# Gelu and GpSimd units of the FFN left out of the last three slots of a fused gated cross-attention layer and put into its end list

## The chip, the cores and the metric

The kernel runs on one core of a Trainium2 chip. A core has five engines that run their own instruction queues and wait for each other with semaphores: TensorE (PE, matrix products, with PEld for its weight loads), VectorE (DVE), ScalarE (ACT), GpSimd (POOL) and SyncE (SP, which here issues all DMA transfers). The metric is the device time of one execution in microseconds (us). Before the change the median of three runs is 2996.57 us, from 2995.82 to 2997.93.

## The reference

One layer of gated cross-attention with a gated, quantised feed-forward network (FFN), on 32 sequences of 224 tokens of width 512. The context has 750 tokens of width 384 for each sequence.

```
x = x + tanh(g_xattn) * attention(layernorm(x), ctx, mask, Wq, Wkv)     # 16 heads of 32
x = x + tanh(g_ffn)   * ffn(layernorm(x), w1, b1, w2, b2)               # 512 -> 2048 -> 512

def bitlinear(x, w, b):
    xq = act_quant(rmsnorm(x))     # each row scaled by its largest value to -128..127, rounded
    wq = weight_quant(w)           # each weight to -1, 0 or 1, by the mean size of all
    return xq @ wq.T + b

ffn(x) = bitlinear(gelu(bitlinear(x, w1, b1)), w2, b2)     # gelu in its exact form
```

The softmax is over the 750 context tokens; a masked query row gets equal weights. Both feed-forward products work on rounded numbers, so before each of them a row needs its root mean square, its largest value and a rounding.

## The kernel before

**Steps and slots.** The attention is cut into 128 steps: 32 sequences times 4 groups of 4 heads. A step has six slots. The three even ones (k = 0, 2, 4) compute the scores for the maxima of the *next* step (`maxima`, line 322), the three odd ones the weights of *this* step (`weights`, line 379). `weights` writes the scores minus the maximum into PSUM (tiles `se`), takes one exponential on ScalarE over 125 x 1792 numbers (tile `p`), and lets GpSimd add the results up (tile `acc`, one addition for u = 0, two for u = 1 and u = 2). There is one PSUM tile for scores, so the scores of slot k + 1 wait until the exponential of slot k has read its own. `minus_max` (line 349) makes the maxima on VectorE after slot 4, and `turn_max` (line 368) turns them with TensorE (tile `pn`) and copies them on ScalarE into `nT`, which the scores of the next step take as an operand. `values` and `sums` (lines 412 and 426) multiply the weights of the step before with the values and add up their sums, both into a tile `po`; `finish` scales the result on GpSimd (tile `yo`) and `store` writes it to `o_d` in memory.

**FFN units.** The FFN works on 28 pairs of 128-row tiles, numbered 0 to 27. `ffn_units` (line 571) cuts a pair into small named units: `load`, `add`, `stats`, `rsqrt`, `norm`, `max`, `sa0` to `sa2`, `grid`, `bias`, `round` and `turn` for the pair, and then for each tile t of two `b` (first product and bias on VectorE, four column blocks, PSUM tiles `ph`), `gelu`, `square`, `hm` (largest value, two halves), `sb0` to `sb2` (scales), `cgrid`, `cround`, `cturn` (a DMA transpose), `c` (second product) and `out`. The numbers of a row go to an integer grid by a multiplication and an added constant (`grid`, `cgrid`), are rounded into bf16 on ScalarE (`round`, `cround`; tiles `xq`, the reused `xc`, and `hq`) and transposed (`xT`, `hT`).

**What orders them.** Every engine works in the order in which the program issues its instructions. In the steps, `Ffn.fill` (line 872) is called once in each slot with the room that is left on TensorE, ScalarE and VectorE, and takes the first units that fit and are `ready` (line 863): a unit must wait some slots after the unit before it and for the units that `behind` names. In the last step but one (n = N - 2 = 126) this is the last call of all. After it `Ffn.drain` (line 910) orders everything that is left, the last step's attention (`top` for `turn_max`, `w0` to `w2`, `val`, `fin0`, `sto0`, `vlast`, `fin1`, `sto1`) among the rest of the FFN units, by a list of costs (`TAKES_US`, line 792). It picks, among what can start within 2 us of the earliest, the unit with the longest work behind it. In the drain a Gelu is held back until the last step's exponentials are issued (line 855), since Gelu and exponential need different tables on ScalarE. In a slot of a step, `b_gelu` (line 686) issues the Gelu and then an exponential of one element a row, `warm`, which brings the exponential's table back:

```
            act.activation(h, h, AF.Gelu)
            if not draining:

                act.activation(warm, magic, AF.Exp)
```

Pairs 26 and 27 use buffers that the attention no longer needs: `xo` for their rows, `wq_sb` and `wkv_sb` for the hidden numbers of pair 26. Names such as `p_3_0` mean the tile p of head group 3 (of the last sequence), u = 0; `h_0` of pair 25 is its tile 0.

Of the kernel before, what the change touches and what calls it, by code (L numbers as in the profile page):

```python
# [24 lines left out]
def flamingo_gated_layer(  # L25
# [18 lines left out]
    class Ordered:  # L44


        def __init__(self, engine):
            self.engine = engine
# [140 lines left out]
    N = len(steps)  # L189
# [178 lines left out]
    def turn_max(n):  # L368
        b, g = steps[n]
        pn = ps_m.tile([P, NQ, CP], BF16, tag="m", name=f"pn_{b}_{g}")  # L370
        for t in range(NQ):
            pe.transpose(
                pn[:, t, :], nbs[n % 2][:, t].rearrange("p j r -> p (j r)"), identb[:CP, :CP]
            )
        nT = smp.tile([P, S], BF16, tag="nT", name=f"nT_{b}_{g}")
        act.copy(nT, pn.rearrange("p t n -> p (t n)"))
        nT_of[b, g] = nT
# [442 lines left out]
        }.items()  # L820
    }

    class Ffn:

        def __init__(self):
            self.slot = 0
            self.parts = []
            self.next = 0  # L830
            self.at = {}

        def behind(self, pair, name):

# [27 lines left out]

        def ready(self, pair, unit):
            name, lag, after = unit[:3]
            lag = lag if not draining else 0
            if after is not None:
                at = self.at.get((pair, after))
                if at is None or self.slot < at + lag:
                    return False
            return all(at in self.at for at in self.behind(pair, name))  # L870
# [39 lines left out]
        def drain(self, more):  # L910

            draining.append(True)
            free = {"PE": 0.0, "ACT": 0.0, "DVE": 4.3, "POOL": 5.0, "SP": 0.0}
            end = {}

            def takes(name):
                kind = name.rstrip("0123456789")
                return TAKES_US.get(kind) or TAKES_US[kind + name[-1]]  # L920

            self.parts.insert(0, [NF, more])
            while self.next < NF:
                self.parts += [[self.next, part] for part in ffn_units(self.next)]
                self.next += 1
            left = {}

            def rank(at):

                if at not in left:  # L930
                    left[at] = 0.0
                    left[at] = sum(us for _, us in takes(at[1])[0]) + max(
                        (rank(x) for x in behind if at in behind[x]), default=0.0
                    )
                return left[at]

            behind = {
                (pair, u[0]): [(pair, u[2] or "")] + self.behind(pair, u[0])
                for pair, units in self.parts for u in units
            }  # L940

            def course(at, way):

                t = max(
                    [end.get(x, 0.0) for x in behind[at]
                     if x[1].rstrip("0123456789") not in ORDER_ONLY or x[1][:-1] != at[1][:-1]],
                    default=0.0,
                )
                t = begin = max(t, free[way[0][0]])
                for engine, us in way:  # L950
                    t = max(t, free[engine]) + us
                return begin, t

            while self.parts:
                self.slot += 10
                found = []
                for part in self.parts:
                    for unit in part[1]:
                        if self.ready(part[0], unit):
                            at = part[0], unit[0]  # L960
                            way = min(
                                takes(unit[0]), key=lambda way: course(at, way)[1]
                                + 1.0 * sum(us for engine, us in way if engine == "DVE"),
                            )
                            found.append((course(at, way)[0], -rank(at), part, unit, way))
                soon = min(f[0] for f in found) + 2
                t, _, part, unit, way = min((f for f in found if f[0] <= soon), key=lambda f: f[1])
                part[1].remove(unit)
                self.at[part[0], unit[0]] = self.slot
                small[0] = {"DVE": dve, "POOL": gp}.get(way[-1][0], act)  # L970
                unit[6]()
                for engine, us in way:
                    t = max(t, free[engine])
                    free[engine] = t + (QUEUE_US[unit[0].rstrip("0123456789")] if engine == "SP" else us)
                    t += us
                end[part[0], unit[0]] = t
                self.parts = [p for p in self.parts if p[1]]
            return end
# [47 lines left out]
    ffn = Ffn()  # L1026
# [5 lines left out]
    for n in range(N - 1):  # L1032
        b, g = steps[n]
        nxt = steps[n + 1]
        last = steps[n - 1] if 0 < n else None
        slots = [[] for _ in range(6)]
        quick = []

        def put(k, us, fn, first=False):
            slots[k].append((us, fn))  # L1040
            if first:
                quick.append(fn)

        def put_values(*ks):

            if v_left:
                at = v_left.pop(0)
                for i, k in enumerate(ks):
                    put(k, 2.7 / len(ks), lambda i=i: v_piece(*at, i if len(ks) > 1 else None))

        put(0, 0.2, lambda: turn_max(n), first=True)
        if last:
            put(2, 2.7, lambda: (values(*last), sums(*last)), first=True)
            put(5, 0.0, lambda: store(*last), first=True)
        if n + 2 < N:
            ks = k_units(*steps[n + 2]) if n else first_k
            if n:
                put(0, 1.9, ks[0])
            put(1, 1.9, ks[1])
        if g == 2 and b + 2 < B:  # L1060
            put(0, 0.0, lambda: load_y(b + 2, 3, 0))
            put(2, 0.0, lambda: load_y(b + 2, 3, 1))
            put(4, 0.0, lambda: load_y(b + 2, 3, 2))
        if g == 3 and b + 2 < B:
            put(0, 0.0, lambda: load_x(b + 2))
        if n in V_MORE:
            put_values(V_MORE[n])
        if n == 0:
            put(3, 1.7, lambda: centre(2 * P, D))
        if n < 2:  # L1070
            put(5, 1.5, q0[n + 2])
        lent = v_left[0] if v_left else None
        put_values(4)
        whole = slots[4][-1][1] if lent else None
        if g < 2:
            put_values(3, 5)
        more = b + 1 < B
        if more and g == 0:
            norm, qs = q_units(b + 1)
            put(0, 0.0, norm[0], first=True)  # L1080
            put(2, 0.0, norm[1], first=True)
            put(4, 0.0, norm[2], first=True)
        if more and g == 1:
            put(1, 0.0, norm[3], first=True)
            put(5, 0.0, lambda: load_xT(b + 1))
        if more and g > 1:
            put(3, 1.5, qs[2 * g - 4])
            put(5, 1.5, qs[2 * g - 3])
        for k in range(6):
            if k % 2 == 0:  # L1090
                maxima(*nxt, k // 2)
            else:
                if k == 3 and last:
                    finish(*last)
                weights(b, g, k // 2)
            if k == 4:
                minus_max(n + 1)

            used = sum(us for us, _ in slots[k])
            early = [unit for us, unit in slots[k] if unit in quick]  # L1100
            for unit in early:
                unit()
            if wunits:
                if k in (1, 3, 5):
                    wunits.pop(0)()
            else:
                some = ffn.fill(
                    (PE_ROOM[k % 2] - used, (1.1, 2.2)[k % 2], 1.7),
                    (n - (k < 5)) // NG if n else 0,
                )  # L1110
                if k == 0 and not some and lent is not None:

                    v_piece(*lent, 0)
                    slots[4] = [
                        (1.35, lambda: v_piece(*lent, 1)) if unit is whole else (us, unit)
                        for us, unit in slots[4]
                    ]
            for us, unit in slots[k]:
                if unit not in quick:
                    unit()  # L1120
# [50 lines left out]
```

## Time and profile before

| what | value |
|---|---|
| median of three runs | 2996.57 us |
| profiled execution: time of its own | 2990.66 us |
| profiled execution: span, first to last instruction | 2988.9 us |
| mean granted clock of TensorE | 0.991 |
| busy: PE, DVE, ACT, POOL | 97%, 58%, 47%, 70% of the span |
| last exponential of step N - 2 | 2888.03 to 2889.69 us |
| last exponential of the last step | 2904.88 to 2906.55 us |

Times in the profile count from the first instruction. Nearly all instructions carry line 52, the helper that records them, so they are told apart by engine and tile names: `p<-se` on ACT is the exponential, `acc<-acc,p` on POOL the sums, `h<-h` on ACT a Gelu, `ACT_TABLE_LOAD` a change of ScalarE's function table. In an order of time a row gives the start, the length, engine, operation, output and input, and in square brackets how long the engine had been idle and what ended that. In the chain of work that ended last, each row is a piece that the end hung on. In a table of stretches, each engine's busy time stands with its number of instructions, in the order PE, PEld, DVE, ACT, POOL; then come the granted TensorE clock, the share of DMA time and GB/s.

The last step and the end list take the last 100 us or so of the span. There TensorE is no longer busy throughout: its wait for transposed tiles of the second FFN product alone comes to 24.4 us after 2889 us.

### The profile page before, as it was taken

Reading aid. Unit: us, or ns where it says so; the run is one execution under the profiler, and the core shown is the slowest. Engines: PE = TensorE matmul, PEld = TensorE weight load, DVE = VectorE, ACT = ScalarE, POOL = GpSimd, SP = SyncE. Lnnn points to the kernel's source line nnn. Section 1 sums busy time; section 2 is a strip of 40 time slices with the busy share of each in tenths; the row PEclk is TensorE's granted clock in tenths of the full one; section 3 lists DMA queues with packets and bytes.
Section 4 is the critical chain, followed back from the end, with each engine's and each line's share of the span. In section 5 each row is a group of like instructions: output and inputs, shape, how many; then the busy total and the mean of one; then the engine's idle time right before and its main releaser. Section 6 shows DMA issues by size and latency. Waiting matters only on the chain.

```text
span 2988.9 us, 62964 instructions
## 1 busy us (share of the span) xinstructions
PE 2891.5 (97%) x26814; PEld 1839.9 (62%) x26814; DVE 1725.5 (58%) x2588; ACT 1417.8 (47%) x1438; POOL 2081.6 (70%) x2727
## 2 busy tenths in 40 slices
PE   8999999999999999999999999999999999999976
PEld 5666566666666666666666666666666666666643
DVE  5576555655555565556555555654655655556545
ACT  2344454544545455445445454553543554545444
POOL 3566767767777777767667777767767777687674
PEclk9999999999999999999999999999999999999987
DMA  5433223123222212221222222223122222321213
GB/s 152 106 95 98 54 57 79 35 59 73 53 58 63 58 48 70 65 68 32 57 72 53 58 61 64 46 58 75 44 49 65 48 69 63 69 74 27 46 45 79
DMA packets 376697, 190.03 MB, mean 64 GB/s; under 512 B 283104, under 2 KB 340576, under 8 KB 376288
## 3 DMA queue, kind: packets, MB, share of 16 engines
q1 hardware_dynamic: 376416, 186.02, 25.8%
q8 instruction: 209, 3.42, 0.5%
q14 instruction: 72, 0.59, 0.1%
HBM read 119.86 MB, written 29.39 MB: 50 GB/s over the span
## 4 chain that ended last, share of the span: by engine, by line
PE 82%; ACT 10%; POOL 3%; DVE 3%; issue 1%; DMA 1%; POOLq 0%; ACTq 0%; SPq 0%; DVEq 0%
PE po L52 17%; PE pk L52 14%; PE se L52 14%; PE sm L52 12%; PE pv_None L52 8%; ACT p L52 7%; PE ph L52 6%; PE pv L52 6%; PE pq L52 3%; DVE mx L52 2%; ACT L52 2%; POOL acc L52 1%; ACT h L52 1%; PE pn L52 1%; POOL r_a L52 1%
## 5 line engine op out<-in xcount | busy, mean ns | idle before, releaser
L52 POOL TENSOR_TENSOR acc<-acc,p 125x896 f32<-125x896 f32 x510 | 1066.0, 2090 | 325.7 <-ACT p L52 304.2
L52 DVE TENSOR_REDUCE mx<-sm 112x4 f32<-112x2000 f32 (+1 forms) x384 | 861.0, 2242 | 664.5 <-PE sm L52 662.6
L52 ACT ACTIVATE p<-se 125x1792 f32<-125x1792 f32 x384 | 639.1, 1664 | 759.0 <-PE se L52 701.6
L52 PE MATMUL pk<-y,wkv_sb 128*128 128x375 f32 x1536 | 538.3, 486 | 2.0 <-DMA y<-in_ctxT 2.0
L52 PE MATMUL sm<-kT,qT 32*112 32x500 f32 (+1 forms) x4096 | 426.7, 508 | 31.6 <-ACT p L52 22.7
L52 POOL TENSOR_TENSOR acc<-p 125x896 f32<-125x896 f32 x128 | 268.3, 2096 | 244.4 <-ACT p L52 244.3
L52 PEld LDWEIGHTS pk<-y,wkv_sb 128*128 128x128 f32 x1536 | 277.8, 189 | 174.4 <-issue 34.5
L52 PE MATMUL se<-qT,kT 32*125 32x224 f32 x6144 | 359.5, 348 | 0.0
L52 PE MATMUL po<-p,v 125*32 125x224 f32 x6144 | 318.1, 355 | 0.0
L52 PE MATMUL pv<-wkv_sb,y 128*125 128x256 f32 x1248 | 311.0, 385 | 0.0
L52 PEld LDWEIGHTS se<-qT,kT 32*125 32x125 f32 x6144 | 295.5, 183 | 0.0
L52 PEld LDWEIGHTS sm<-kT,qT 32*112 32x112 f32 x4096 | 159.2, 170 | 190.1 <-ACT p L52 138.7
L52 PEld LDWEIGHTS po<-p,v 125*32 125x32 f32 x6144 | 186.9, 110 | 119.5 <-issue 44.0
L52 PEld LDWEIGHTS pv<-wkv_sb,y 128*125 128x125 f32 x1248 | 223.2, 188 | 52.3 <-issue 17.8
L52 ACT COPY kT<-pk 128x375 f32<-128x375 f32 x256 | 120.3, 470 | 278.8 <-PE pk L52 278.0
L52 PE MATMUL pv_None<-wkv_sb,y 128*125 128x256 f32 x1056 | 250.9, 387 | 0.0
L52 PEld LDWEIGHTS pv_None<-wkv_sb,y 128*125 128x125 f32 x1056 | 191.2, 187 | 89.0 <-issue 59.7
L52 PE MATMUL po<-w2q,hT 128*128 128x256 fp8e4 x1792 | 222.1, 280 | 24.4 <-DMA hT<-hq 24.4
L52 DVE SCALAR_TENSOR_TENSOR h<-ph,qa_am,b_sb 128x512 f32<-128x512 f32 x216 | 158.9, 745 | 139.0 <-PE ph L52 111.1
L52 PE MATMUL ph<-w1q,xT 128*128 128x512 fp8e4 x896 | 226.1, 384 | 4.8 <-DMA xT<-xc 4.8
L52 PE MATMUL pq<-xTb,wq_sb 128*128 128x224 f32 x1024 | 221.4, 359 | 0.4 <-DVE wq_sb L52 0.4
L52 PEld LDWEIGHTS <-hT 128*128 128x128 bf16 x1792 | 171.8, 100 | 76.6 <-issue 27.1
(131 smaller groups left out, 2863.1 us busy)
## 6 DMA issues: line engine op xcount, KB each, us to landing
y<-in_ctxT SPq DMA_DIRECT2D x90, 375.0 KB, 4.7
x<-in_x SPq DMA_DIRECT2D x32, 448.0 KB, 4.0
xTb<-in_xT SPq DMA_DIRECT2D x32, 448.0 KB, 3.7
o_d<-yo SPq DMA_DIRECT2D x512, 28.0 KB, 1.9
xg<-in_x SPq DMA_DIRECT2D x26, 512.0 KB, 3.8
og<-o_d SPq DMA_DIRECT2D x26, 512.0 KB, 4.4
out<-xg SPq DMA_DIRECT2D x52, 256.0 KB, 2.2
wa<-in_w1T SPq DMA_DIRECT2D x8, 512.0 KB, 5.6
```

Source lines behind the costliest of these rows:

```text
L52: return lambda *args, **kw: tc.keep_in_program_order(build(*args, **kw))
```

## The change

In the slots k = 3, 4 and 5 of the step n = N - 2, a unit whose name without its digits is in `NOT_LAST` is not ready. It stays in the list of the FFN and is ordered by the drain instead. The flag is cleared when the drain begins. The names are Gelu and units that run on GpSimd. Nothing is left out of the computation.

```
+    NOT_LAST = "gelu", "add", "rsqrt", "grid", "bias", "cgrid", "sb"
...
     class Ffn:
...
             self.at = {}
+            self.closing = False
...
         def ready(self, pair, unit):
             name, lag, after = unit[:3]
+            if self.closing and name.rstrip("0123456789") in NOT_LAST:
+                return False
...
             draining.append(True)
+            self.closing = False
...
             else:
+                ffn.closing = n == N - 2 and k > 2
                 some = ffn.fill(
```

More of the change, by code (lines that the diff above doesn't have):

```diff
@@ L821, in flamingo_gated_layer @@
     }
+    NOT_LAST = "gelu", "add", "rsqrt", "grid", "bias", "cgrid", "sb"
     class Ffn:
@@ L831, in __init__ @@
             self.at = {}
+            self.closing = False
         def behind(self, pair, name):
@@ L864, in ready @@
             name, lag, after = unit[:3]
+            if self.closing and name.rstrip("0123456789") in NOT_LAST:
+                return False
             lag = lag if not draining else 0
@@ L914, in drain @@
             draining.append(True)
+            self.closing = False
             free = {"PE": 0.0, "ACT": 0.0, "DVE": 4.3, "POOL": 5.0, "SP": 0.0}
@@ L1106, in flamingo_gated_layer @@
             else:
+                ffn.closing = n == N - 2 and k > 2
                 some = ffn.fill(
```

## The prediction

> **What bounds the kernel now.** The page comes first. TensorE (PE) is busy for 97% of the span, but an average can hide the end, and the change touches only the last step, so the second view is the chain of work that ended last, from 2888 us on. The third is each engine's order of time over the last 100 us, the fourth a table of stretches with the granted clock.
>
> From the page:
>
> ```profile
> span 2988.9 us, 62964 instructions
> PE 2891.5 (97%) x26814; PEld 1839.9 (62%) x26814; DVE 1725.5 (58%) x2588; ACT 1417.8 (47%) x1438; POOL 2081.6 (70%) x2727
> ```
>
> From the chain (start, us, what):
>
> ```profile
> 2888.03 1.66 ACT p L52
> 2889.71 1.28 ACT L52
> 2891.00 1.91 ACT h L52
> 2892.93 1.28 ACT L52
> 2894.22 0.20 ACT warm L52
> 2894.43 0.24 ACT nT L52
> 2894.71 2.13 PE se L52 x19
> ...
> 2903.66 2.08 POOL acc L52
> ...
> 2910.07 1.37 POOL xc L52 x2
> ...
> 2911.46 1.16 ACT xc L52
> 2912.64 2.42 DMA xT<-xc
> ```
>
> The reader is to see that between the last exponential of step N-2 and the first scores of the last step the chain runs through ScalarE (ACT) alone: a table load, the Gelu of one FFN tile, a table load back, the one-element exponential, and only then the copy nT that the scores wait for. After that it runs over the sums of the weights on GpSimd (POOL) to the quantisation of pair 26 there, and from this through ACT and a DMA to PE.
>
> From PE's, POOL's and ACT's order of time:
>
> ```profile
> 2886.73 0.41 PE L52 MATMUL se<-nT,ones 3*125 3x448 bf16 x4 [0.53 <-DVE mx L52]
> 2889.57 0.26 PE L52 MATMUL pn<-identb,nb 112*128 112x112 bf16 x2
> 2894.71 0.64 PE L52 MATMUL se<-nT,ones 3*125 3x448 bf16 x4 [4.88 <-ACT nT L52]
> 2900.07 0.55 PE L52 MATMUL po<-acc,ones 125*32 125x224 f32 x8
> 2889.83 4.23 POOL L52 TENSOR_TENSOR acc<-acc,p 125x896 f32<-125x896 f32 x2 [2.24 <-ACT p L52]
> 2911.46 1.15 ACT L52 ACTIVATE xc<-xc,magic 128x1024 bf16<-128x1024 f32 x1 [4.92 <-POOL xc L52]
> ```
>
> PE turned the maxima (pn) by 2889.83 and then sat for 4.88 us until nT came. The scores after this idle are slow, 0.64 us where 2886.73 shows 0.41 for the same four matmuls. The stretches say why: in the column PEclk (the fraction after the five engines) the clock is 1.00, and half of that after the idle.
>
> ```profile
> 2886.00:2890.00 4.00, 3.30 (x31) 1.97 (x31) 3.79 (x11) 1.96 (x2) 1.76 (x2) 1.00 0.27 106
> 2895.00:2898.00 3.00, 3.00 (x36) 1.93 (x35) 0.00 (x0) 1.03 (x1) 0.00 (x0) 0.50 0.00 0
> ```
>
> **The change part by part.** Compared engine by engine, the built programs say what moves. POOL's and SP's queues are the same, instruction for instruction: no GpSimd unit, no transfer and no store changes place, so six of the seven names in NOT_LAST do nothing here. What moves is one Gelu, tile 0 of pair 25, and what hangs on it.
>
> *1. ACT, ahead of nT.* Taken away: two table loads (1.28 each), the Gelu (1.91) and the one-element exponential (0.20): with their gaps 4.6 us, from 2889.71 to the copy at 2894.33. With ACT free at 2889.69 the copy waits for pn, 2889.83 as PE's row ends, and takes its 0.33: nT is there at 2890.2 and not at 2894.66, so scores 3_0 start at 2890.25, 4.45 earlier.
>
> *2. The cold start of scores 3_0.* Cold, the exponential starts 2.26 after the scores (2894.71 to 2896.97), warm 1.30 (2886.73 to 2888.03; 2900.55 to 2901.85). In the new order PE has been idle for 0.4 us only, so I take 1.30: p_3_0 runs from 2891.55 to 2893.2, 5.4 earlier. The other end is 2.26, if the clock falls all the same.
>
> *3. What is late next.* The 48 matmuls of po_2 take 2.3 us warm (the row at 2877.46 against 3.47 here), so they end at 2893.65. The sums behind them need acc_2 of POOL, which the change doesn't move: 2889.83 + 4.23 = 2894.06. So PE waits some 0.45 us in a place where it did not wait before. Scores 3_1, 0.48 behind those sums as before (2900.07 to 2900.55), begin at 2894.6 instead of 2900.55: 5.95 earlier. This bound absorbs small errors in the first two terms; it stays if nT is up to 0.4 us later than I have it.
>
> *4. To pair 26.* p_3_1 ends 1.30 + 1.66 behind, at 2897.56 (was 2903.52); acc_3 adds its two halves on POOL until 2901.98 (was 2907.93; POOL has done acc_3's first part by 2896.3). Then POOL's same list runs: yo_2, the scales, the grid of pair 26, which ended at 2911.43 and will at 2905.48. It is 5.95 again.
>
> *5. Where the Gelu goes.* It now stands on ACT between p_3_2 (ends 2900.6 instead of 2906.55) and the rounding of pair 26. Load and Gelu are 1.28 + 1.91 + gaps = 3.25, so ACT is free at 2903.85, 1.65 ahead of the grid: what covers it is the idle of 4.92 us at 2911.46. Without that cover it would cost 3.25. The later load before the Gelu of tile 1 (1.28 at 2914.52) falls away, since Gelu's table stays; nothing waits for that Gelu closely.
>
> *6. Other places that shift.* On PE po_3 goes ahead of ph_1_2, four matmuls of 1.04 that lay beside the wait for p_3_2. Both are done by 2905.2, and PE then idles for the transpose of pair 26 (now landing at 2909.15): nothing. On DVE, ph_1_2's bias goes behind oT_3, and both maxima of the moved Gelu (2 x 1.2) ahead of ph_1_3's bias, which ends at 2908.2; tile 1's Gelu starts at 2908.6 and with its square is through by 2912.6, ahead of pair 26's Gelu (2922.48 - 5.95 = 2916.5). Covered by 3.9 us. On DVE the last bias of pair 26 (0.75) goes behind the 11 small operations of tile 0's scales (2924.95 to 2927.33). DVE's sum up to the statistics of pair 27 stays the same, so POOL's chain behind them (nm at 2929.04, the roots, the grid, h at 2942.12) keeps 5.95; but the Gelu in wkv_sb, its square, the normalising of pair 27 and the rounding hq_0 come about 1 us late against that: 5 us earlier only. The maxima of pair 27 then end at (in the old times) 2933.6, needed by POOL at 2934.5: 0.9 us of cover. hq_0's transpose makes po_25_0 and the ph of pair 27 about 1 us late too; these ended at 2948.4 and PE then waited 2.1 us for hq_1's transpose, which follows POOL: 1 us of cover is left.
>
> From there on, hq_1, transpose, po_25_1, the Gelus of pair 27 and the four last transposes stand in the same order on every queue, so all of it shifts by the same time.
>
> **Sum.** 4.45 (ACT) + 0.95 (clock) + 1.0 (po_2 warm) - 0.45 (wait for acc_2) = 5.95 us, all on the path. The profiled execution took 2990.66 (span 2988.9 and 1.76 around it), so 2984.7 for such an execution. The median of the runs shown, 2996.57, lies 5.9 above the profiled one; I take the same 5.95 off it: 2990.6, or 0.199% less. Bounds: term 2 cold gives a gain of 4.45 at least up to p_3_0, and po_2 slow too, so 4.5; the upper end is the first rival, 6.9. 0.2% of this kernel, 6.0 us, is about what a measurement can tell from no change, and the forecast lies on that line.
>
> **Rivals.**
>
> *Pair 26 starts warm (gain 6.9, 2989.7).* PE's idle before the ph of pair 26 falls from 4.80 to about 3.9 us. In the old run the first result of it reached DVE 2.0 us after the start (2915.10 to 2917.09) at clock 0.50, warm that would be 1.1. DVE's statistics then come 0.9 earlier, where POOL's addition of pair 27 (ends 2926.34, statistics 2927.25) stops the gain. Against it: an idle of 2.9 us (2971.88 to 2974.77) was enough for clock 0.50; one of 2.1 (2948.4 to 2950.5) was not. 3.9 lies beyond both, so I take cold.
>
> [...]
>
> *The clock falls anyway, or the small covers break (gain 2 to 4.7, about 2993).* Either scores 3_0 still run at half clock, for which only a warm stretch from 2874 to 2890 speaks against, or the 0.9 and 1.0 us of part 6 do not hold. hq_0's transpose would now be in flight when pair 27's begins (old times 2934.4 + 4.3 = 2938.7 against 2938.72), and if the two take turns up to 2.4 us are lost, less the cover.
>
> *Slower.* One mechanism: DVE's new order. The Gelu in wkv_sb now waits for the 11 small operations of tile 0, and these for the square and both maxima of the moved Gelu. As I work it out these stand at 2908.6 and the operations start at 2918.1, so 9.5 us are free. If they came later than that, each further us would go through wkv_sb, pair 27's normalising and POOL to the end, and 6 us more would eat the gain: it decides at 15.5 us, and at 22 the kernel would take 3003. Nothing between 2900 and 2908 on ACT is that long.
>
> *The edit does nothing.* Excluded: the built ACT program has two table loads and the exponential less, and nT directly behind p_2_2.
>
> **How the numbers follow.** The forecast (gain 5.3 to 6.5) has 0.72; about 0.42 of it I put past the line of 6.0 and 0.30 short of it, since the sum falls on the line and the covers taken at their full price leave a little unused (PE's wait for acc_2, DVE's last bias). Warm pair 26: 0.13, past the line. Clock or covers: 0.11, within. Slower: 0.04 by over 0.2%. So 0.55 faster, 0.41 within, 0.04 slower. The range takes in 4.5 as well as 6.9, and the spread of the old runs (0.75 below the median, 1.36 above) with some more for other runs: 2988.0 to 2994.0.
>
> **What would show it.** On ACT nT straight behind the exponential of step N-2, PE's idle before scores 3_0 near 0.4 us and not 4.88, these scores at clock 1.00 (0.41 and about 0.93 us); a new wait of PE for acc_2; p_3_1 ending near 2897.6; ACT's idle before the rounding of pair 26 falling from 4.92 to about 1.7, still ended by POOL; 0.50 at the start of pair 26. I am wrong if the rounding is ended by ACT itself, if the ph of pair 27 run into the transpose of hq_1, or if DVE's scales wait for the square.

## The result and the profile after

The changed kernel takes 2987.5 us (median of 11 runs, 2985.22 to 2989.63) against 2995.46 us (11 runs, 2990.89 to 2997.93) for the kernel before: ratio 0.9975, 95% interval 0.9966 to 0.9984. That is faster by 8.0 us, where 5.95 was forecast, and 0.5 us below the range given. The profiled execution of the changed kernel took 2987.37 us, only 3.3 us less than that of the kernel before (2990.66). So the two kinds of numbers, 8.0 and 3.3, lie on either side of the forecast, and both have to be explained.

The first lines are the page of the changed kernel.

```profile
span 2985.6 us, 62960 instructions
PE 2891.3 (97%) x26814; PEld 1839.3 (62%) x26814; DVE 1726.3 (58%) x2588; ACT 1414.3 (47%) x1435; POOL 2086.4 (70%) x2727
```

Busy times say nothing here. ScalarE in order of time shows the change itself (start, length, engine, what, and in brackets the idle time ahead with what ended it):

```profile
2891.14 1.67 ACT L52 ACTIVATE p<-se 125x1792 f32<-125x1792 f32 x1 [3.60 <-PE se L52]
2892.99 0.34 ACT L52 COPY nT<-pn 128x224 bf16<-128x224 bf16 x1 [0.18 <-PE pn L52]
2894.68 1.66 ACT L52 ACTIVATE p<-se 125x1792 f32<-125x1792 f32 x1 [1.34 <-PE se L52]
...
2903.93 1.28 ACT L52 ACT_TABLE_LOAD   x1
2905.22 1.91 ACT L52 ACTIVATE h<-h 128x2048 f32<-128x2048 f32 x1
2908.71 1.15 ACT L52 ACTIVATE xc<-xc,magic 128x1024 bf16<-128x1024 f32 x1 [1.58 <-POOL xc L52]
```

nT stands straight behind the last exponential of step N-2. The table load and the Gelu lie behind the last exponential of the last step, and the rounding of pair 26 behind them still waits for GpSimd, 1.58 us instead of 4.92.

TensorE in order of time:

```profile
2893.39 0.41 PE L52 MATMUL se<-nT,ones 3*125 3x448 bf16 x4 [0.43 <-ACT nT L52]
2893.57 0.98 PE L52 MATMUL se<-qT,kT 32*125 32x224 f32 x16
2894.48 2.48 PE L52 MATMUL po<-p,v 125*32 125x224 f32 x48
2897.28 0.59 PE L52 MATMUL po<-acc,ones 125*32 125x224 f32 x8 [0.32 <-POOL acc L52]
```

The wait for nT is 0.43 us instead of 4.88, the scores run at full clock, and the new wait for GpSimd's sums is there with 0.32 us.

The chain of work that ended last shows what is late next. It no longer passes ScalarE's table loads but GpSimd's sums, and further on the way of the last attention result through memory, which stood beside the chain before:

```profile
2892.95 2.10 POOL acc L52
2895.11 2.12 POOL acc L52
2897.28 0.59 PE po L52 x8
...
2914.03 3.39 DMA o_d<-yo
2917.62 3.96 DMA xo<-o_d
2921.72 2.36 POOL xo L52
2924.10 0.70 DVE st L52
```

Why 3.3 in the one pair of profiles and 8.0 in the medians? The program is the same up to the last exponential of step N-2, and its end is a good place to cut both executions. The kernel before has 2889.69 us ahead of that cut and 99.2 behind it (to the end of the span), the changed kernel 2892.81 and 92.8. So behind the cut the change saves 6.4 us, and ahead of it, in a program that is the same, 3.1 us got lost in this pair.

### The profile page after: what moved, and what is told of

The parts are those of the page before. It is cut to its first block, busy times and chain, and to the rows that moved or that the text cites. A ratio compares the mean times of both kernels' runs of the same rounds, so it can differ in the third digit from the quotient of the medians.

```text
span 2985.6 us, 62960 instructions
## 1 busy us (share of the span) xinstructions
PE 2891.3 (97%) x26814; PEld 1839.3 (62%) x26814; DVE 1726.3 (58%) x2588; ACT 1414.3 (47%) x1435; POOL 2086.4 (70%) x2727
## 4 chain that ended last, share of the span: by engine, by line
PE 83%; ACT 10%; POOL 3%; DVE 2%; issue 1%; DMA 1%; SPq 0%; POOLq 0%; ACTq 0%; DVEq 0%
PE po L52 17%; PE pk L52 15%; PE se L52 14%; PE sm L52 13%; PE pv_None L52 8%; ACT p L52 7%; PE pv L52 6%; PE ph L52 6%; PE pq L52 3%; DVE mx L52 2%; ACT L52 1%; POOL acc L52 1%; ACT h L52 1%; PE pn L52 1%; POOL h L52 1%
```

## The experiments

All cuts below are made at that place, at the end of the fourth last exponential. The traces also record the stretches in which TensorE was granted half the clock; their starts are counted from the cut, except in the first table, where they are counted from the first instruction. The tail is what lies behind the cut.

**The kernel before and the changed kernel again**

No edit.

> The kernel before, unchanged, profiled once more. Cut at the end of the last exponential of step N-2, the first profile has 2889.7 us ahead of it and 99.2 behind it; the changed kernel has 2892.8 and 92.8. Theory A: the change saves 6.4 us behind the cut in every execution, and what lies ahead of the cut scatters by some 7 us from one execution to the next (the first profile was a low one), so that the median of 8.0 saved is 6.4 plus scatter. Then this run has 98.5 to 100 us behind the cut and anything from 2889 to 2897 ahead of it. Rival B: the first profile was low behind the cut too, and a usual execution of the kernel before has 100.5 to 102 us behind it. Rival C: the part ahead of the cut is longer in the kernel before, for a reason in its program: then it would be over 2893 in both repeats.

> The kernel before, unchanged, a third profile. As for the second: theory A 98.5 to 100 us behind the cut, rival B 100.5 to 102, rival C over 2893 us ahead of the cut in both.

> The changed kernel, unchanged, profiled once more. Theory A: 92.3 to 93.5 us behind the cut (first profile 92.8), 2890 to 2896 ahead of it. Rival B, by which the two tails differ by 8: 91 to 92.5 as a usual value. Rival C: ahead of the cut some 2 us less than the two repeats of the kernel before.

Measured, with the third profile of the changed kernel from the run after these (the spans are split as said):

```
                 ahead of the cut   behind it   half clock in the first 2800 us, at (long, us)
before               2889.7           99.2      none
before, 2nd          2890.0           99.2      none
before, 3rd          2894.3           98.9      at 33 (6.8), at 476 (3.4)
changed              2892.8           92.8      at 35 (3.4), at 475 (3.4)
changed, 2nd         2889.5           92.4      none
changed, 3rd         2893.7           95.5      at 32 (6.8)
```

Theory A holds for the kernel before: 98.9 to 99.2 behind the cut, while the part ahead of it lies between 2889.7 and 2894.3. Rival B falls: no tail of the kernel before is over 99.2. Rival C falls as a fixed difference: both programs have executions near 2889.6 and executions over 2892 ahead of the cut. What makes these longer is for the larger part half clock in the first 500 us, 3.4 or 6.8 us in one piece: with none of it the part ahead of the cut takes 2889.5 to 2890.0, with one or two pieces 2892.8 to 2894.3. Followed from one exponential to the next, a piece of 3.4 us costs 1.6 to 1.7 us and one of 6.8 costs 3.0 to 3.1. The rest of the differences, at most 1.1 us at a place, arises in the first 30 us, between 216 and 251 us, and behind 600 us, where the six executions differ by up to 0.5 us. (One more stretch, 10.2 us long and 28 us ahead of the cut, is in all six.)

But the saving is not the same in every execution, as theory A had it. The changed kernel's second execution agrees with it behind the cut and lies 0.5 us below its range ahead of the cut; the third has 95.5 behind the cut where 92.4 to 92.8 were expected. The first two tails save 6.1 to 6.8 us, the third 3.4 to 3.7.

The last product of the third execution explains its longer tail, as TensorE's order of time shows, the second profile of these lines being that execution and the first the one shown above:

```profile
2971.69 3.67 PE L52 MATMUL po<-w2q,hT 128*128 128x256 fp8e4 x32 [3.15 <-DMA hT<-hq]
2978.30 3.67 PE L52 MATMUL po<-w2q,hT 128*128 128x256 fp8e4 x32 [2.94 <-DMA hT<-hq]
```

```profile
2972.35 3.67 PE L52 MATMUL po<-w2q,hT 128*128 128x256 fp8e4 x32 [3.04 <-DMA hT<-hq]
2979.04 6.50 PE L52 MATMUL po<-w2q,hT 128*128 128x256 fp8e4 x32 [3.03 <-DMA hT<-hq]
```

The same wait of 3 us left the clock up in one execution and not in the other, and the last product took 2.8 us more. (Where the two waits differ is shown below, where the falls of the clock are counted.) In the kernel before this didn't happen in the profiles taken: there the product ahead of it ran at half clock itself (6.57 us), lay beside the wait for the last transpose and left only 0.23 us of idle time:

```profile
2974.77 6.57 PE L52 MATMUL po<-w2q,hT 128*128 128x256 fp8e4 x32 [2.91 <-DMA hT<-hq]
2981.57 3.67 PE L52 MATMUL po<-w2q,hT 128*128 128x256 fp8e4 x32 [0.23 <-DMA hT<-hq]
```

**Five more rounds of the pair**

No edit.

> The changed kernel, unchanged, timed against the kernel before in five rounds on one chip. Theory A (the change is worth 6.5 us behind the cut, which is the mean of the tails 99.2, 99.2, 98.9 less 92.8, 92.4; what lies ahead of the cut only scatters): a difference of the medians of 4.5 to 8.5, as the scatter ahead of the cut falls, and over all runs together nearer to 6.5 than to 8. Rival C (something ahead of the cut became shorter too, by 1.5): 8 again. The profile: 92.4 to 92.8 us behind the cut.

Measured: 2988.70 us (11 runs) against 2993.76 (21 runs), ratio 0.9981 (0.9972 to 0.9990): 5.1 us less. Both sets of runs together, 22 and 32 of them, give medians of 2988.27 and 2994.73: 6.5 us less, ratio 0.9978, 0.9974 to 0.9983 from resampling these runs. The two sets, 8.0 and 5.1, lie on both sides of it, and rival C has no support in the second set; why the first set gave just 8.0 is not settled, since of its runs only one of each kernel has a trace.

**The clock behind the wait, alone**

The kernel before, with TensorE kept busy while nT is made:

```
     def turn_max(n):
...
+        if n == N - 1:
+            busy = ps_m.tile([P, 512], F32, tag="m", name="busy")
+            for _ in range(17):
+                pe.matmul(busy, identb, w1q[:, 0, :512], start=True, stop=True)
         nT = smp.tile([P, S], BF16, tag="nT", name=f"nT_{b}_{g}")
```

> The kernel before, with 17 matmuls of 128x512 on data that nobody reads put behind the last turn of the maxima, so that TensorE is busy for about 4.4 of the 4.88 us in which it waits for nT. The wait itself stays; only the clock behind it should. By my terms the clock was worth 0.95 (scores 3_0) and 1.0 us (po_2), and nothing of POOL stands in the way here, so 97.2 us behind the cut, with the scores 3_0 at 0.41 and 0.93 us. The rival, that the clock is worth nothing to the end since POOL's sums bound it: 99.2. If the clock is worth more than I put it: under 96.7.

Measured: 96.5 behind the cut, 2989.79 us, which is under the 96.7 below which the clock would be worth more than I put it. TensorE's order of time:

```profile
2891.19 3.83 PE L52 MATMUL busy<-w1q,identb 128*128 128x512 fp8e4 x17
2896.23 0.41 PE L52 MATMUL se<-nT,ones 3*125 3x448 bf16 x4 [1.21 <-ACT nT L52]
2896.42 0.98 PE L52 MATMUL se<-qT,kT 32*125 32x224 f32 x16
2897.32 2.48 PE L52 MATMUL po<-p,v 125*32 125x224 f32 x48
```

nT comes 4.97 us behind the cut, as in the kernel before, but the first exponential of the last step starts at 6.31 instead of 7.28, the second at 10.21 instead of 12.16, and the rounding of pair 26 at 19.8 instead of 21.8. So the clock behind the wait is worth 0.97 and 0.98 us (0.95 and 1.0 were in the sum), and all of it reaches the rounding. A further 0.6 us comes behind that: the statistics of pair 27 end at 36.7 instead of 39.3, for the half-speed stretch at the first product of pair 26 is 3.4 us long instead of 6.8, and the product takes 8.56 us instead of 9.15.

**The table loads, alone**

The kernel before, with the function of this one Gelu left out, so that ScalarE needs no other table:

```
-            act.activation(h, h, AF.Gelu)
+            act.activation(h, h, AF.Identity if i == 25 and t == 0 else AF.Gelu)
```

> The kernel before, where the one Gelu that the change moves is an identity (its function is left out), so that both table loads ahead of nT fall away and 1.9 + 0.2 us of ScalarE's work stay. nT comes 2.57 us earlier, and TensorE's wait falls from 4.88 to 2.3 us. Theory: the clock stays up (2.1 us left it up, 2.9 did not), which gives 1.95 more, and GpSimd's sums bound nothing: 4.6 us less, 94.0 to 94.7 behind the cut. Rival: the clock falls all the same, 2.6 less: 96.5.

Measured: 95.6 behind the cut, 2990.03 us: 0.9 away from the theory and from the rival, but the clock fell, as the rival has it.

```profile
2892.49 0.26 PE L52 MATMUL pn<-identb,nb 112*128 112x112 bf16 x2
2894.78 0.64 PE L52 MATMUL se<-nT,ones 3*125 3x448 bf16 x4 [2.03 <-ACT nT L52]
2895.11 1.80 PE L52 MATMUL se<-qT,kT 32*125 32x224 f32 x16
2896.85 3.11 PE L52 MATMUL po<-p,v 125*32 125x224 f32 x48
```

The clock fell after a wait of 2.03 us, shorter than the 2.13 us which left it up in the first profile of the kernel before. So the length of a wait of 2 to 3 us doesn't decide it; my reading that the limit lies between 2.1 and 2.9 was wrong, and so was the theory here. Half the clock for 3.4 us cost here most of the two clock terms: the rounding of pair 26 starts 3.2 us earlier than in the kernel before, against 2.8 for nT alone and 5.9 in the changed kernel.

**The cover of the moved Gelu used up**

The changed kernel with two more squares behind the moved Gelu:

```
             act.activation(h, h, AF.Gelu)
+            if i == 25 and t == 0:
+                for e in range(2):
+                    extra = fp.tile([P, F], BF16, tag="junk", name=f"extra_{e}")
+                    act.activation(extra, h, AF.Square)
```

> The changed kernel with two more squares of 128x2048 on ScalarE directly behind the moved Gelu, 3.85 us of work whose result nobody reads. They use up the 1.58 us that ScalarE waits there for GpSimd's grid. Theory: the rounding of pair 26 starts 2.3 us later, ended by ScalarE's own work, and the kernel is 2.3 us longer: 94.8 behind the cut. Rival: the rounding of pair 26 is not what the end hangs on: 92.6.

Measured: the rounding starts at 18.0 instead of 15.9 and has no idle time ahead of it; 95.5 behind the cut, 2.7 to 3.1 more than the two quicker tails of the changed kernel.

```profile
2906.94 3.85 ACT L52 ACTIVATE extra<-h 128x2048 bf16<-128x2048 f32 x2
2910.70 1.13 ACT L52 ACTIVATE xc<-xc,magic 128x1024 bf16<-128x1024 f32 x1
```

So 3.85 us of work cost 2.1 us at the rounding: the rest lay in the cover. The end moved by somewhat more, as half-speed stretches fall otherwise (the one at the first product of pair 26 is 6.8 us long instead of 3.4, and the product takes 9.24 us instead of 8.53 to 8.75). The end alone would prove little, since the third execution of the changed kernel has a tail of 95.5 as well. But there it is the last product that is slow, and here the delay is there all the way: the statistics of pair 27 end at 35.4 instead of 32.6 to 33.0, and the second products of pair 26 begin 2.4 to 2.8 us later. So the end does hang on this rounding.

**Pair 26's grid on VectorE**

```
-            free = {"PE": 0.0, "ACT": 0.0, "DVE": 4.3, "POOL": 5.0, "SP": 0.0}
+            free = {"PE": 0.0, "ACT": 0.0, "DVE": 4.3, "POOL": 9.0, "SP": 0.0}
```

> The changed kernel with one number of the end list's planner changed: GpSimd counts as free from 9 us on, not from 5. By that VectorE does the scales and the grid of pair 26 (it idles for 6.2 us ahead of them), and nothing else changes place. In the changed kernel the rounding of pair 26 waits 1.58 us for GpSimd's grid after the moved Gelu. Theory: then the Gelu itself ends this wait, the rounding starts 1.5 us earlier, at 14.4 us behind the cut, and the kernel is 1.5 us shorter: 91.1 behind the cut. Rival: the sums of GpSimd and the additions of pair 27 behind them bound the end in any case: no gain, 92.6.

Measured: the rounding starts at 14.1 and the statistics of pair 27 end at 30.6, 1.8 and 2.0 to 2.4 earlier than in the changed kernel. But at the end 92.1 us are behind the cut, 0.3 to 0.7 less than the quicker tails there, and nearer to the rival's 92.6 than to the theory's 91.1. In five rounds 2987.87 us against 2993.76, ratio 0.9980 (0.9970 to 0.9989), which can't be told from the changed kernel on the same chip (2988.70). TensorE's order of time shows where most of the gain went, first here and then in the changed kernel:

```profile
2936.92 6.38 PE L52 MATMUL ph<-w1q,xT 128*128 128x512 fp8e4 x28
2946.29 2.45 PE L52 MATMUL po<-w2q,hT 128*128 128x256 fp8e4 x16 [2.99 <-DMA hT<-hq]
2948.53 1.91 PE L52 MATMUL ph<-w1q,xT 128*128 128x512 fp8e4 x4
```

```profile
2947.47 1.92 PE L52 MATMUL po<-w2q,hT 128*128 128x256 fp8e4 x16 [2.32 <-DMA hT<-hq]
2949.23 1.03 PE L52 MATMUL ph<-w1q,xT 128*128 128x512 fp8e4 x4
```

The changed kernel has 1.92 and 1.03 us for these two, behind a wait of 2.32. Here the wait is 2.99, the clock falls, and 1.4 us go. A wait made longer by a gain can so give the gain back to the clock.

**TensorE's waits of the end list filled**

```
+        def hold(us):
+            if not us:
+                return
+            busy = ps_s.tile([P, HG, 512], F32, tag="s", name="busy")
+            for _ in range(int(us / 0.215)):
+                pe.matmul(busy[:, 0, :], identb, w1q[:, 0, :512], start=True, stop=True)
...
         def b_matmul(t, f):
+            if (i, t, f) == (26, 0, 0):
+                hold(3.0)
...
         def c_matmul(t, half):
+            if half == 0:
+                hold({(25, 0): 13.0, (25, 1): 1.8, (26, 0): 5.2, (27, 0): 2.8, (27, 1): 2.6}.get((i, t), 0))
```

> The changed kernel with matmuls of 128x512 on data that nobody reads, 0.215 us each, put into six waits of TensorE in the end list, each batch some 0.3 to 1.4 us shorter than the wait that the changed kernel shows there: 3.0 us ahead of the first product of pair 26, 13.0 and 1.8 ahead of the second products of pair 25, 5.2 ahead of those of pair 26, 2.8 and 2.6 ahead of those of pair 27. Nothing else moves. Theory (the clock is what is left of the scatter behind the cut): no half-speed stretch from 9 us behind the cut on, the second products of pair 26 take 7.4 and not 9.2 us, which is on the path, and the last product is never slow; 90.3 to 91.0 us behind the cut, and a median 2 to 3 us below the changed kernel's 2988.3. Rival: the stretches lie beside waits for transposes, the end does not move: 92.4 to 92.8.

> The same filled waits, and pair 26's scales and grid on VectorE as in the earlier run. There the rounding of pair 26 started 1.8 us earlier and the statistics of pair 27 ended 2.2 us earlier, but at the end 0.3 to 0.6 of it was left: TensorE waited 2.99 us ahead of po_25_1, the clock fell there and po_25_1 and the ph behind it took 1.4 us longer. Theory: with that wait filled the 2.2 us stay to the end, 88.2 to 89.0 us behind the cut, 4 us below the changed kernel. Rival: the gain was lost to the transposes or the order of the queues, not to the clock: 90.0 to 90.8, as without the grid on VectorE.

Measured: the changed kernel with filled waits has 90.5 us behind the cut, and of half clock only the 3.4 us at 9 and what comes after the last matmul. The second products of pair 26 take 3.67 us each, where the changed kernel needs 9.17 for both:

```profile
2958.79 3.67 PE L52 MATMUL po<-w2q,hT 128*128 128x256 fp8e4 x32 [0.47 <-DMA hT<-hq]
2963.79 3.67 PE L52 MATMUL po<-w2q,hT 128*128 128x256 fp8e4 x32 [1.33 <-DMA hT<-hq]
2967.30 2.97 PE L52 MATMUL busy<-w1q,identb 128*128 128x512 fp8e4 x13
2970.10 3.66 PE L52 MATMUL po<-w2q,hT 128*128 128x256 fp8e4 x32
```

Median 2986.32 us (8 runs) against 2994.38 (12 runs), ratio 0.9971 (0.9961 to 0.9982), 2.0 us below the 2988.27 of the changed kernel. With the grid on VectorE as well it is 89.9 behind the cut and 2985.20 us (5 runs), ratio 0.9969 (0.9956 to 0.9981). Against the kernel before in the same runs that is 8.1 and 9.2 us less, where the changed kernel's runs have 6.5, but the intervals overlap with that of the changed kernel. The first of the two expectations came true. In the second the theory (88.2 to 89.0) was missed by 0.9 us and the rival (90.0 to 90.8) by 0.1: only 0.6 of the 2.2 us came through. The statistics of pair 27 end at 30.6 with the grid on VectorE, filled waits or not, and filled waits alone bring them to 31.2. So the two gains cover the same place to a large part.

## Why the prediction was wrong in its range and right in its mechanism

**Part 1, ACT ahead of nT: right.** nT is done 0.53 us behind the cut instead of 4.97: 4.44, forecast 4.45. **Part 2, the cold start: right.** The first exponential starts 1.87 behind the cut instead of 7.28, 5.41 earlier (5.4); alone it measured 0.97 (0.95). **Part 3, what is late next: right.** TensorE waited 0.32 us for acc_2 (0.45), and the second exponential comes 5.87 earlier (5.95). **Part 4, to pair 26: right.** acc_3 ends 5.88 earlier and the rounding starts 5.87 earlier. **Part 5, the cover: right.** 1.58 us are left (1.65), and with the cover used up the end moves. **Part 6, the other places:** the pieces off the path stayed off it, and the first product of pair 26 still started cold, as in the forecast, though behind 3.37 us of idle time and not about 3.9.

**What was missing from the sum.** I put pair 26 either cold as before or warm. It was cold, but in a half-speed stretch of 3.4 us instead of 6.8: the product takes 8.56 us instead of 9.15. The order of time and the stretches (the granted clock stands behind the five engines), before and after:

```profile
2915.10 9.15 PE L52 MATMUL ph<-w1q,xT 128*128 128x512 fp8e4 x32 [4.80 <-DMA xT<-xc]
2915.10:2919.10 4.00, 4.00 (x10) 1.50 (x11) 1.12 (x2) 3.96 (x3) 0.00 (x0) 0.50 0.38 66
```

```profile
2912.35 8.56 PE L52 MATMUL ph<-w1q,xT 128*128 128x512 fp8e4 x32 [3.37 <-DMA xT<-xc]
2912.30:2916.30 4.00, 3.95 (x12) 1.56 (x13) 1.28 (x2) 3.47 (x3) 0.00 (x0) 0.61 0.38 65
```

So the statistics of pair 27 end 6.3 to 6.7 earlier than in the first profile of the kernel before, and behind the cut 6.4 to 6.8 us less are left in the two quicker executions of the changed kernel. About half of the first rival's gain came true. In the first of them the statistics also waited 0.30 us for GpSimd's addition for pair 27, the stop that this rival named. In a third execution the last product took 2.8 us more: the wait ahead of it, which I took over unchanged (0.23 us in the kernel before), is now 3 us. That one I had not seen: I moved all four last transposes together and did not ask at which clock the products between them would run.

**The step that failed** is the base of the sum: "The median of the runs shown, 2996.57, lies 5.9 above the profiled one; I take the same 5.95 off it: 2990.6". Three runs had a median of 2996.57, and 32 runs have one of 2994.73: 1.8 us of the miss of 3.1 are in this number. Within the first set of 11 runs the base is 1.1 too high (2995.46), and the other 2.0 are its saving of 8.0 against 5.95, which lies inside the interval of that saving (4.8 to 10.2). The part ahead of the cut scatters by 4 to 5 us from one execution to the next, and I gave the lower end of the range only 1.7 us below the 2989.7 of the largest gain: the 0.75 from the median to the lowest of three runs, and some more. With the larger set as a base the same 5.95 would give 2988.8, and the 22 runs of the changed kernel have a median of 2988.27; the 0.8 from there to the 2987.5 of the first set are scatter of its runs. The saving itself was sized well: 5.95 against 6.5 (medians of all runs) and 6.24 (means; 95% interval 5.3 to 7.1).

**The rivals.** The slower one had no place: the square and the maxima were done 9 us ahead of the scales that wait for them (2911.8 and 2920.8). Of the clock falling anyway, scores 3_0 show nothing, and the covers held; the part of the trace that spoke against it, a warm stretch ahead, held too. But the clock did fall once in a new place, for 3.4 us at 9 us behind the cut, in all three executions of the changed kernel, behind a wait of 1.85 us:

```profile
2900.81 0.41 PE L52 MATMUL se<-nT,ones 3*125 3x448 bf16 x4 [1.85 <-ACT p L52]
2901.00 1.10 PE L52 MATMUL se<-qT,kT 32*125 32x224 f32 x16
2902.03 3.98 PE L52 MATMUL po<-p,v 125*32 125x224 f32 x48
```

The po_3 in the last line took 2.48 us in the kernel before. It cost nothing here, as TensorE then waits 3.37 us for the transpose of pair 26.

**When the clock fell.** The granted clock in these runs is 1.00 or 0.50, and the half-speed stretches that end within an execution last 3.4, 6.8, 10.2 or 13.7 us, all multiples of 3.41; within an execution their starts lie such multiples apart too. Waits of 1.85, 2.03, 2.99 and 3.03 us brought the clock down here, and other waits of 2.13, 2.32, 2.94 and 3.15 did not, so the length of a wait alone doesn't decide it.

The traces show where these waits differ. Each trace was cut into slices of 3.41 us, counted from the starts of its half-speed stretches, and TensorE's rows give the time in each slice in which no matmul ran. In the twelve traces 10311 slices at full clock have a successor on record. All 66 with more than 2.01 us idle are followed by half clock, and none of the 10214 with less than 1.72; of the 31 between, 14 are and 17 are not, and what decides there stays open. Of all these slices 1714 are in the first profiles of the two kernels, where half clock follows all 11 above, none of the 1700 below and 2 of the 3 between. So in these traces the fall goes with how much of a wait lies in one slice. The last wait of the changed kernel's first execution, 2.94 us, is split into 1.47 and 1.47; that of the third, 3.03 us, has 2.05 in one slice. The 2.13 us of the kernel before have at most 1.66 in one, the 2.03 us without the table loads 2.02. No run moved a wait against the slices, so this is read from the traces alone.

## What to carry to other kernels

An engine's stall that leaves TensorE idle can cost twice: in the kernel before, TensorE waited 4.88 us for ScalarE and then ran at half clock for 4.1 us, and 4.4 us of ScalarE's work cost 5.9 at the next point that all of it hung on. When an edit near the end is costed, cut the profiles at the last point that both programs share and compare what lies behind it; the scatter ahead of it (4 to 5 us here) was as large as the effect, and a median of three runs is no base for a range of 6 us. Ask of each wait that gets longer by a gain whether the matmuls behind it will still find the clock up: here half clock followed all 66 of the 3.41 us slices that held more than 2.01 us of idle time.

## What the runs showed that was not expected

- A wait of about 3 us ahead of the same product left the clock up in two of three executions of the changed kernel and not in the third, where the product took 6.50 us instead of 3.67. It had 2.05 us in one slice of 3.41 us in the third, and at most 1.47 and 1.96 in the other two.
- Most of the scatter ahead of the cut sits in the first 500 us: 3.4 or 6.8 us at half clock near 33 us (start of the steps) and 3.4 near 476 us, or none, in the same program.
- Matmuls that nobody needs made the kernel shorter: 17 of them in one wait took 2.4 to 2.7 us off the tail of the kernel before, and 130 in six waits took 1.9 us or more off that of the changed kernel.
